# A list scheduler's price for changing the tensor engine's array mode, and new due times, in a four-layer transformer kernel

## The chip, the cores and the metric

The kernel runs on one core of a Trainium2 chip. The metric is the device time of the program in microseconds; the time of a kernel is the median of several runs. The engines are called TensorE (PE), VectorE (DVE), ScalarE (ACT), GpSimd (POOL) and SyncE (SP, which issues transfers); PEld is the loading of weights into TensorE.

## The reference

Eight sequences of 512 x 512 numbers pass through four layers. Each layer is `x = x + layernorm(f(layernorm(x)))`, with these four functions `f`:

```python
# 1: attention without weights, on each of the 8 sequences
weights = softmax(einsum('bci,bcj->bij', x, x)); out = einsum('bij,bcj->bci', weights, x)
# 2: eight 512 x 512 factors, summed by linearity, then a bias
out = einsum('btd,rde->bte', x, factors) / sqrt(8) + bias
# 3: RMS norm, 8 query heads of 64 in 2 groups that share keys and values, output projection
h = norm_scale * x / (norm(x) / sqrt(512) + eps) * split_scale
q, k, v = h @ Wq.T, h @ Wk.T, h @ Wv.T
out = x + softmax(q @ k.T / 8) @ v @ Wo.T
# 4: gated feed-forward with 1408 hidden units and ternary weights
out = (silu(x @ gate_w.T * gate_s) * (x @ up_w.T * up_s)) @ down_w.T * down_s
```

All numbers are float32.

## The kernel before

The 8 sequences are called batches 0 to 7. Each has four token tiles of 128 rows. Per batch there are four stages: `stage_attn0` (names that begin with a0), `stage_ffn0` (f0), `stage_attn1` (a1; for the last batch its attention rows, products and projections are named e1) and `stage_ffn1` (f1; h1 for the last batch, where the first gate products are split into two halves of the tokens). TensorE does the following in them:

- a0: transposes of the normalized x (L635), the upper half of the score matrix (L693, and transposes L691 for the rest), transposes of the softmax rows (L635), context products (L724).
- f0, for each token tile: four transposes of a normalized row (L609), eight matmul instructions against the summed factors (L746).
- a1: transposes (L635), keys (L885), values (L896), queries (L915); then, for four pairs of heads and two halves of the tokens, scores (L944), transposes of the softmax rows (L975), attention products (L1006), and the output projections (L1032).
- f1: transposes (L635), gate and up products (L1165, eight instructions each), down products (L1233).

TensorE works in four modes, by which the planner tells operations apart: "128x128" is whole float32 work (L609, L693, L724, L746, L885, L896, L915, L1032), "64x128" is work on two halves of the array's rows (L635, L944, L975), "128x64" on two halves of its columns (L1006), and "128x128r" is whole work on float32r operands (L1165, L1233). In float32r a value is split into two parts, which are multiplied by weights that are exact in it. A flag that is computed from the weights' low bits (the "low" loads and L463) tells whether this holds; otherwise the whole program runs again in float32.

No order of instructions is written out by hand. Each stage hands its operations to a `Recorder` with an engine, an estimated duration, the buffers that it reads and writes, and a priority. `Recorder.issue` then puts them in order: again and again it looks, for each engine, at the operations that could start within SLACK of the earliest, and takes the one with the smallest due time. An operation that needs another mode than the engine is in starts later by `Recorder.change`, and its due time counts as later by STAY times that. The order so found is the order in each engine's queue[...]. Due times come from `due`: the table DUE holds for each kind of work a start and steps, in units of one batch, and SHIFT adds an offset for a stage and a batch; SMALL is taken off for operations under 0.3 us.

Buffers are rings: 5 banks f and 3 banks g of PSUM, 4 tiles e for softmax rows, 3 tiles row, 2 tiles hl, and 4 tiles each of ws (weights of a1, loaded on SP's queue) and wgu (gate and up weights, loaded on POOL's queue, L387). A buffer is taken when the operation that first needs it is put in order, so that order also decides when loads can start. The statistics of a normalization take DVE (L516, L521), then POOL (L525, L532), then DVE again (L540); the addition to x is on POOL (L559).

Of the kernel before, what the change touches and what calls it, by code (L numbers as in the profile page):

```python
# [53 lines left out]
class Recorder:  # L54
# [4 lines left out]
    @staticmethod  # L59
    def change(eng, old, new):  # L60


        if new is None or new == old:
            return 0.0
        if eng == "ACT":
            return 1.3
        return 0.09 * (old is None or old.strip("r") != new.strip("r")) + 0.12 * new.endswith("r")

    def __init__(self):
        self.ops = []  # L70
# [2 lines left out]
    def add(self, eng, dur, fn, reads=(), writes=(), room=(), after=(), state=None, lat=None):  # L73
# [5 lines left out]
        op.lat = self.LAT[eng] if lat is None else lat  # L79
        op.prio = self.prio - (SMALL if dur < 0.3 else 0.0)  # L80
        op.succ, op.wait, op.ready = [], 0, 0.0
# [34 lines left out]
    def issue(self, places, slack):  # L116
# [24 lines left out]
        while left:  # L141
            best = None
            for e, ops in ready.items():
# [3 lines left out]
                first = min(able)[0]  # L147
                stay = STAY.get(e, 0.0)
                pick = min(
# [99 lines left out]
def layers(  # L249
# [1034 lines left out]
    with tc.manual_schedule():  # L1284
        rec.issue(places, SLACK)

# [1 line left out]


DUE = {  # L1290
    "x": (-2.595,),
    "fsum": (0.4631, 0.0036),
    "scales": (-1.7557,),
    "wd": (0.2919,),
    "low": (0.8154, 1.1722),
    "a0.norm": (0.602,),
    "a0.row": (-0.0133, 0.0064),
    "a0.out": (0.6155, 0.0012),
    "f0": (-0.2291, 0.103),
    "a1.norm": (0.498, -0.0333),  # L1300
    "a1.kv": (-2.1194,),
    "a1.q": (0.5487, 0.0684),
    "a1.row": (0.5193, 0.0805, 0.0215, -0.0006),
    "a1.mix": (1.3287, 0.0052, 0.0124),
    "a1.out": (1.6207, -0.0361),
    "e1.row": (0.4681, -0.0113, 0.0525, -0.0529),
    "e1.mix": (-2.4837, 58.3341, 0.0746),
    "e1.out": (1.1439, 0.155, 0.0456),
    "f1.norm": (-0.1878, 0.009),
    "f1.gate": (1.5586, 0.0013),  # L1310
    "f1.down": (1.7415, 0.1322, 0.0313),
    "h1.norm": (1.5393, -1.0876, 0.0495),
    "h1.gate": (2.1757, 0.4491, 4.54),
    "h1.down": (1.6071, -1.5421, 1.3412),
}

SHIFT = {
    ("a0", 0): 0.0119,
    ("a1", 0): -0.3641,
    ("f0", 0): 0.0009,  # L1320
    ("f1", 0): -0.1337,
    ("x", 0): 0.0116,
    ("a0", 1): 0.0009,
    ("a1", 1): -0.1282,
    ("f0", 1): -0.3583,
    ("f1", 1): -0.001,
    ("x", 1): 0.0094,
    ("a0", 2): 0.0721,
    ("f1", 2): -0.0021,
    ("x", 2): 0.3533,  # L1330
    ("a1", -2): -0.0219,
    ("f0", -2): -0.0106,
    ("f1", -2): -0.0418,
    ("x", -2): -0.0328,
    ("a0", -1): 0.0045,
    ("a1", -1): -0.1019,
    ("f0", -1): 0.0436,
    ("f1", -1): 0.0947,
}

STAY = {"PE": 0.1755}

SLACK = {"PE": 0.123, "ACT": 0.0985, "DVE": 0.0676, "POOL": 0.7848, "SP": 0.1357}

SMALL = 0.8265
FSUM_POOL = (0, 3)
EARLY = (-1,)
FEW = 4
# [54 lines left out]
```

## Time and profile before

| | us |
|---|---|
| median of 3 runs | 1516.56 (1516.08 to 1517.06) |
| profiled execution | 1518.21 |
| its span, first to last instruction | 1516.3 |
| TensorE busy in it | 1472.7 |
| VectorE busy | 1052.4 |
| ScalarE busy | 671.1 |
| GpSimd busy | 578.6 |
| first matmul starts at | 15.9 |
| last matmul ends at | 1506.7 |

The span leaves 1.9 us of the profiled execution around it. "Busy" is the union of an engine's instructions; for TensorE the ends of matmuls are modelled, so idle time that the profile shows on it is a lower bound of what it lost. In a timeline, each line gives the start, the length, the engine, the line of the program, the operation with what it writes and reads, the number of merged instructions, and in brackets the idle time before it and what ended that. In a list of waits, the numbers are the total, the count and the longest.

### The profile page before, as it was taken

To read this page: it belongs to the slowest core of one execution; us is meant where nothing else is said; L and a number is where in the kernel's file an instruction comes from. 1 tells how busy PE (TensorE), PEld (TensorE's weight loads), DVE (VectorE), ACT (ScalarE), POOL (GpSimd) and SP (SyncE) were. 2 spreads that over 40 slices of the span, in tenths; PEclk is the share of its full clock that TensorE was granted. 3 is DMA by queue.
4 is the path that set the end of the run, shared out by engine and by line. 5 is a ranking of instruction groups with operands and counts; after the bars stand their busy time and mean duration, and the time that the engine had idled before them with its cause. 6 is when DMAs were issued, how large, how long until landed. Compare 5 with 4: busy or idle time off the path is not lost.

```text
span 1516.3 us, 23151 instructions
## 1 busy us (share of the span) xinstructions
PE 1472.7 (97%) x8562; PEld 909.2 (60%) x8562; DVE 1052.4 (69%) x2227; ACT 671.1 (44%) x1426; POOL 578.6 (38%) x884
## 2 busy tenths in 40 slices
PE   5999999999999999999999999999999999999997
PEld 3444557655766557665566656665566655666575
DVE  6899865768558685586846868466774757748745
ACT  3226645642276414663256622565325642266312
POOL 6661142236412374033721347103571116602341
PEclk9999999999999999999999999999999999999999
DMA  9523046112521214212151122411233103420281
GB/s 335 158 84 112 2 105 112 36 42 49 98 63 43 48 44 91 56 48 65 29 104 36 57 56 49 97 37 43 56 70 84 36 15 77 77 63 22 56 161 38
DMA packets 156698, 108.04 MB, mean 71 GB/s; under 512 B 7072, under 2 KB 137120, under 8 KB 156576
## 3 DMA queue, kind: packets, MB, share of 16 engines
q0 software_dynamic: 98736, 51.13, 17.9%
q1 hardware_dynamic: 57840, 55.34, 11.5%
q8 instruction: 70, 1.15, 0.3%
q14 instruction: 52, 0.43, 0.1%
HBM read 98.06 MB, written 8.39 MB: 70 GB/s over the span
## 4 chain that ended last, share of the span: by engine, by line
PE 80%; DVE 9%; POOL 6%; DMA 2%; issue 2%; SPq 0%; ACT 0%; POOLq 0%; DVEq 0%; ACTq 0%
PE g L1165 18%; PE g L1233 11%; PE f L944 7%; PE f L1006 7%; PE f L915 7%; PE f L1032 6%; PE f L724 6%; PE f L975 5%; PE f L693 4%; PE f L746 3%; PE f L635 2%; POOL rstd L532 2%; PE f L896 2%; PE f L885 2%; DVE row L540 1%
## 5 line engine op out<-in xcount | busy, mean ns | idle before, releaser
L1165 PE MATMUL g<-hl,wgu 128*128 128x512 f32 (+1 forms) x1408 | 339.3, 394 | 1.9 <-DMA wgu<-in_gate_t 1.7
L1165 PEld LDWEIGHTS g<-hl,wgu 128*128 128x128 f32 x1408 | 256.7, 189 | 71.9 <-DVE s L573 10.6
L525 POOL TENSOR_SCALAR ve<-mv 128x1 f32<-128x1 f32 x224 | 62.5, 280 | 591.6 <-DVE mv L521 584.4
L573 DVE TENSOR_REDUCE s<-f 128x1 f32<-128x512 f32 x288 | 184.9, 684 | 107.3 <-PE f L944 66.5
L580 ACT ACTIVATE e<-f,s 128x512 f32<-128x512 f32 x288 | 195.9, 688 | 76.5 <-DVE s L573 73.3
L559 POOL TENSOR_TENSOR x<-x,z 128x512 f32<-128x512 f32 x120 | 163.8, 1368 | 48.2 <-DVE z L540 42.7
L1233 PE MATMUL g<-wd,hl 128*128 128x512 f32 x704 | 174.8, 401 | 1.4 <-DVE hl L1108 1.4
L987 ACT COPY big<-f 128x512 f32<-128x512 f32 x256 | 135.9, 593 | 71.8 <-PE f L975 71.5
L1233 PEld LDWEIGHTS g<-wd,hl 128*128 128x128 f32 x704 | 129.4, 188 | 52.3 <-issue 20.7
L597 DVE TENSOR_SCALAR e<-e,s 128x512 f32<-128x512 f32 x288 | 145.3, 508 | 8.4
L532 POOL TENSOR_TENSOR rstd<-ve,mhalf 128x1 f32<-128x1 f32 x224 | 142.0, 638 | 16.0
L387 POOL DMA_DIRECT2D wgu<-in_up_t x92 | 75.0, 815 | 151.1 <-PE g L1165 146.6
L944 PE MATMUL f<-kv,big 64*128 64x512 f32 x512 | 131.2, 613 | 0.1
L1195 DVE SCALAR_TENSOR_TENSOR sig<-g,gs,sig 128x512 f32<-128x512 f32 x84 | 62.7, 747 | 87.4 <-ACT sig L1185 87.1
L1006 PE MATMUL f<-big,kv 128*64 128x256 f32 x1024 | 122.6, 384 | 0.0
L1032 PE MATMUL f<-ws,big 128*128 128x512 f32 x256 | 116.6, 600 | 0.7 <-ACT big L870 0.7
L746 PE MATMUL f<-fsum,rT 128*128 128x512 f32 x256 | 115.7, 595 | 0.2
L915 PE MATMUL f<-big,ws 128*128 128x512 f32 x256 | 115.5, 599 | 0.0
L724 PE MATMUL f<-big,big 128*128 128x512 f32 x256 | 114.8, 597 | 0.0
L1185 ACT ACTIVATE sig<-g,gs 128x512 f32<-128x512 f32 x84 | 58.6, 698 | 119.4 <-PE g L1165 99.6
L387 POOL DMA_DIRECT2D wgu<-in_gate_t x92 | 72.6, 790 | 99.9 <-PE g L1165 93.3
L1204 DVE SCALAR_TENSOR_TENSOR hd<-g,us,sig 128x512 f32<-128x512 f32 x84 | 62.8, 747 | 67.0 <-PE g L1165 63.8
(91 smaller groups left out, 1920.2 us busy)
## 6 DMA issues: line engine op xcount, KB each, us to landing
wgu<-in_gate_t POOLq DMA_DIRECT2D x92, 256.0 KB, 3.3
wgu<-in_up_t POOLq DMA_DIRECT2D x92, 256.0 KB, 3.3
x<-in_x SPq DMA_DIRECT2D x32, 256.0 KB, 2.6
ws<-in_wq_t SPq DMA_DIRECT2D x32, 256.0 KB, 3.3
ws<-in_wo_t SPq DMA_DIRECT2D x32, 256.0 KB, 2.6
out<-x SPq DMA_DIRECT2D x32, 256.0 KB, 2.0
hd<-in_factors SPq DMA_DIRECT2D x28, 256.0 KB, 5.3
wd<-in_down_t POOLq DMA_DIRECT2D x11, 256.0 KB, 8.4
```

The source lines that it names most:

```text
L532: lambda: nc.gpsimd.tensor_tensor(rstd.t[:, :], ve.t[:, :], mhalf, ALU.pow),
L559: lambda: on.tensor_tensor(ap(xt), ap(xt), y.t[:, :], ALU.add),
L573: lambda: nc.vector.tensor_reduce(nmax.t[:, :], sc.t[:, :], AX.X, ALU.max, negate=True),
L580: lambda: nc.scalar.activation(e.t[:, :], sc.t[:, :], AF.Exp, bias=nmax.t[:, :], accum_out=tot.t[:, :]),
L724: nc.tensor.matmul(po.t[:, :], xnT.t[:, j, ts(t, P)], wT.t[:, j, :], start=(j == 0), stop=(j == KT - 1),)
L746: nc.tensor.matmul(po.t[:, :], xnT.t[:, kt, :], fsum.t[:, kt, :], start=(kt == 0), stop=(kt == KT - 1),)
L915: nc.tensor.matmul(pq.t[:, :], wq.t[:, kt, :], hT.t[:, kt, :], start=(kt == 0), stop=(kt == KT - 1),)
L944: nc.tensor.matmul(scs[g].t[:, :], qT.t[gp, i, ts(s, P)], kT.t[gp, :], start=True, stop=True,)
L1006: nc.tensor.matmul(po.t[gp, : 2 * P], v.t[:, t * P + g * DH : t * P + (g + 1) * DH], columns_of(aT)[:, g * NT + t, :], start=(t == 0), sto ...
L1032: nc.tensor.matmul(po.t[:, :], qT.t[:, i, ts(t, P)], flat(wos[i].t), start=(i == 0), stop=(i == NPAIR - 1),)
L1165: nc.tensor.matmul(bank.t[:, cut], w.t[:, kt, :], d.t[:, kt, cut], start=(n == 0), stop=(n == KT * len(xs) - 1),)
L1233: nc.tensor.matmul(po.t[:, :], ap(o)[:, it - lo, :], wd.t[:, it, :], start=(it == 0 and k == 0), stop=(it == NI - 1 and k == len(ops) - 1),)
```

## The change

The function that prices a change of mode on TensorE is given other prices. Before, a change between "128x128" and "128x128r" cost 0.12 us into float32r and 0 out of it, a change from tiled work to float32r cost 0.21, and any other change 0.09. After, a change between "128x128" and "128x128r" costs 0 in both directions, and every other change costs 0.21 into float32r and 0.09 elsewhere. All due times, the offsets by batch, STAY, three of the SLACK values and SMALL get new values. No operation, buffer, duration or transfer is added or taken away. The line numbers of the kernel after are larger by 2 from L67 on.

```diff
-        return 0.09 * (old is None or old.strip("r") != new.strip("r")) + 0.12 * new.endswith("r")
+        if old is not None and old.strip("r") == new.strip("r"):
+            return 0.0
+        return 0.21 if new.endswith("r") else 0.09
...
-    "f0": (-0.2291, 0.103),
-    "a1.norm": (0.498, -0.0333),
-    "a1.kv": (-2.1194,),
-    "a1.q": (0.5487, 0.0684),
-    "a1.row": (0.5193, 0.0805, 0.0215, -0.0006),
-    "a1.mix": (1.3287, 0.0052, 0.0124),
...
+    "f0": (-0.1636, 0.1196),
+    "a1.norm": (0.4967, -0.0502),
+    "a1.kv": (-1.8548,),
+    "a1.q": (0.5431, 0.0591),
+    "a1.row": (0.5193, 0.0765, 0.0294, -0.0187),
+    "a1.mix": (1.4217, -0.005, 0.0185),
...
-STAY = {"PE": 0.1755}
-
-SLACK = {"PE": 0.123, "ACT": 0.0985, "DVE": 0.0676, "POOL": 0.7848, "SP": 0.1357}
-
-SMALL = 0.8265
+STAY = {"PE": 0.0901}
+
+SLACK = {"PE": 0.123, "ACT": 0.0528, "DVE": 0.0772, "POOL": 1.2606, "SP": 0.1357}
+
+SMALL = 0.8159
```

The other entries of DUE and SHIFT change in the same manner.

More of the change, by code (lines that the diff above doesn't have):

```diff
@@ L1290 @@
 DUE = {
[L1291 to L1298, printed above, removed]
-    "f0": (-0.2291, 0.103),
-    "a1.norm": (0.498, -0.0333),
-    "a1.kv": (-2.1194,),
-    "a1.q": (0.5487, 0.0684),
-    "a1.row": (0.5193, 0.0805, 0.0215, -0.0006),
-    "a1.mix": (1.3287, 0.0052, 0.0124),
-    "a1.out": (1.6207, -0.0361),
-    "e1.row": (0.4681, -0.0113, 0.0525, -0.0529),
@@ L1307 @@
[L1307 to L1314, printed above, removed]
+    "x": (-2.3159,),
+    "fsum": (0.3241, 0.0093),
+    "scales": (-1.7199,),
+    "wd": (0.1588,),
+    "low": (0.6749, 1.0396),
+    "a0.norm": (0.5999,),
+    "a0.row": (-0.0925, 0.0032),
@@ new lines @@
+    "a0.out": (0.61, 0.0014),
+    "f0": (-0.1636, 0.1196),
[4 more added lines that the diff above has]
+    "a1.mix": (1.4217, -0.005, 0.0185),
+    "a1.out": (1.6212, -0.0623),
+    "e1.row": (0.2868, -0.0014, 0.037, -0.0171),
+    "e1.mix": (-2.6369, 42.9472, 0.5484),
+    "e1.out": (1.0638, 0.0783, 0.0342),
+    "f1.norm": (-0.7064, 0.0727),
+    "f1.gate": (1.5542, 0.001),
+    "f1.down": (1.7443, 0.1972, 0.0317),
@@ L1315 @@
+    "h1.norm": (1.3712, -0.2677, 0.0575),
+    "h1.gate": (2.6762, 0.5726, 5.4087),
+    "h1.down": (1.5597, -2.5384, 1.2861),
 }
 SHIFT = {
[L1318 to L1338, printed above, removed]
-}
-STAY = {"PE": 0.1755}
-SLACK = {"PE": 0.123, "ACT": 0.0985, "DVE": 0.0676, "POOL": 0.7848, "SP": 0.1357}
-SMALL = 0.8265
+    ("a0", 0): -0.0077,
+    ("f0", 0): 0.3239,
+    ("f1", 0): -0.0869,
+    ("a0", 1): -0.1846,
+    ("a1", 1): -0.1496,
+    ("f0", 1): -0.3089,
+    ("x", 1): -0.0564,
+    ("a0", 2): 0.3238,
+    ("a1", 2): -0.0022,
+    ("f0", 2): 0.0353,
@@ L1346 @@
+    ("f1", 2): -0.0044,
+    ("x", 2): 0.0586,
+    ("a1", -2): -0.0031,
+    ("f0", -2): 0.1802,
+    ("f1", -2): -0.0946,
+    ("x", -2): -0.3405,
+    ("a0", -1): -0.0302,
+    ("a1", -1): -0.1096,
+    ("f0", -1): -0.4004,
+    ("f1", -1): -0.1873,
+    ("x", -1): 0.1371,
+}
+STAY = {"PE": 0.0901}
+SLACK = {"PE": 0.123, "ACT": 0.0528, "DVE": 0.0772, "POOL": 1.2606, "SP": 0.1357}
+SMALL = 0.8159
 FSUM_POOL = (0, 3)
```

## The prediction

> **What bounds the kernel now.** I read the page first: busy shares, granted clock, chain.
>
> ```profile
> span 1516.3 us, 23151 instructions
> PE 1472.7 (97%) x8562; PEld 909.2 (60%) x8562; DVE 1052.4 (69%) x2227; ACT 671.1 (44%) x1426; POOL 578.6 (38%) x884
> ...
> PEclk9999999999999999999999999999999999999999
> ...
> PE 80%; DVE 9%; POOL 6%; DMA 2%; issue 2%; SPq 0%; ACT 0%; POOLq 0%; DVEq 0%; ACTq 0%
> ```
>
> TensorE (PE) is busy 97% of the span, at full clock in every slice, and is most of the chain. The span is therefore PE's work, plus what a change of array mode costs, plus PE's waits. The diff leaves the matmuls alone, so only the last two can move. Next, PE's waits over the span, and the places where the largest stand in the PE timeline:
>
> ```profile
> PE f L635 <- DVE big L540: 15.9, 1, 15.9
> PE f L609 <- DVE row L540: 4.2, 6, 0.9
> PE f L635 <- DVE z L540: 2.0, 2, 1.6
> PE g L1165 <- DMA wgu<-in_gate_t: 1.7, 3, 0.9
> ```
>
> ```profile
> 558.62 2.07 PE L1165 MATMUL g<-hl,wgu 128*128 128x512 f32 x8
> 560.53 3.59 PE L746 MATMUL f<-fsum,rT 128*128 128x512 f32 x8
> 564.99 0.66 PE L609 MATMUL f<-ident,row 128*128 128x128 f32 x4 [0.86 <-DVE row L540]
> ```
>
> ```profile
> 164.80 1.11 PE L944 MATMUL f<-kv,big 64*128 64x512 f32 x4
> 165.71 0.22 PE L975 MATMUL f<-ident,e 64*128 64x64 f32 x1
> 166.13 1.01 PE L975 MATMUL f<-ident,e 64*128 64x64 f32 x15 [0.20 <-ACT big L987]
> 166.98 2.29 PE L944 MATMUL f<-kv,big 64*128 64x512 f32 x4
> 169.20 1.95 PE L1006 MATMUL f<-big,kv 128*64 128x256 f32 x16
> ```
>
> 15.9 us is the start, before the first operand. Ends of matmuls are modelled, so I measure a wait from start to start. At 560.53 a feed-forward product of the first layer (L746) takes 4.46 us until the next transposes start, where others take 3.43 to 3.58: a loss of 0.95 (0.86 shown as idle). It recurs in batches 3, 4, 5 and 6 (564.99, 748.41, 931.51, 1114.58): 3.8 us. In the second fence, two score products (L944) keep PE 2.22 us instead of 1.03, because the product behind them (L1006) waits for copies; no idle is printed, since the modelled end is stretched. Six such places between 159 and 179 us lose 0.35, 0.86, 0.72, 1.19, 0.86 and 0.76: 4.7 us.
>
> [...] Over all neighbours in the PE timeline, start to start less what the same products take among their like, a change from tiled work (64x128 or 128x64) to float32r costs 0.23 us, tiled to whole 0.20, float32r or whole to tiled 0.15, between the two tilings 0.15 to 0.17; between whole float32 and float32r it is 0.00 to 0.02. [...] after the start no wait is above 1.6 us and the granted clock is 0.996, so the clock is no second lever. [...] L540 took 1.55 us beside a GpSimd add (L559, 1.26 us from 563.39), against 0.57 for the rows of the later normalization.
>
> **The change part by part.** It edits no instruction; it alters the planner's price of a PE mode change, due times, STAY, SLACK and SMALL, and all of these act through the order alone. I compared the two orders, engine by engine. PE's first 37 operations are the same, and its last 47 (from 1419.5 us on: the last attention products and projections, the split gates, the last down products). So the 15.9 us start, the other waits before 97 us, the waits for wgu near the end and the 1.36 us one at 1484 stay. SP keeps 203 of 215 places and moves no entry by more than 7; POOL's wgu loads keep their sequence, four of them stand earlier between its small operations near 1420 us.
>
> *Mode changes.* Before: 461; 67 between whole and float32r (free), 394 paid. After: 470; 75 free, 395 paid. By kind: tiled to float32r 71 to 72 (+0.23 us); tiled to whole 82 to 82; 128x64 to 64x128 49 to 47 (-0.3), 64x128 to 128x64 40 to 41 (+0.2); float32r to tiled 75 to 72 (-0.45), whole to tiled 77 to 81 (+0.6). Sum +0.3. Priced by single lines rather than by mode, I get -0.6. I take 0, range -0.6 to +0.3. The new price is nearer to the measured ones, but its effect on the number of paid changes is nil.
>
> *First feed-forward, batches 2 to 7.* The row of the fourth token tile hangs on the last context product (L724) through two normalizations on DVE and POOL. I add up the PE work between that product and the transposes that need the row (cover). Before: 17.5 us in batches 3 to 6, which stall; 21.5 and 21.1 in batches 2 and 7, which don't. After: two gate products (L1165, 1.9 each) move ahead of these transposes, cover is 21.1 in batches 3 to 7, and 17.5 in batch 2. Four losses go, one comes: -3 x 0.95 = -2.85. What is late next: in the new order DVE writes the row only after the bias (0.68) and statistics (0.69, 0.18) of the third tile, so about 2.1 to 3.6 us after the third product (the row at 0.57 or at 1.55), against 3.8 us of gate products. It fits barely: at worst 0.3 each, +1.5.
>
> *Attention of batch 0, 159 to 179 us (4.7 us lost).* Feed-forward products, keys of batch 1 and transposes are interleaved with it otherwise. Covers in the new order: an attention product (L1006) behind its transposes has 1.1 us once and 1.6 twice (before, 1.1 three times, losing 0.86, 1.19, 0.86, so about 2.0 is needed): +0.9 and +0.4; the other 1.6 follows the wait named next, which covers it. One set of softmax transposes (L975) stands only 1.0 us behind its scores; before, 3.5 was the shortest and did not stall: up to +2.5. The values' weights (wv, L896) reload a ws buffer that the keys (L885) free, with 2.6 us of PE work between; ws loads land 2.5 to 5.8 us after issue, median 2.8, and the SP queue has nothing unfinished ahead: about +0.4. Sum 4.2 against 4.7: -0.5. Bounds: -3 if the softmax is covered by what PE has already waited for, +2.5 if as much again is exposed.
>
> *Batch 2 (339 to 361 us).* Transposes of batch 3 (L635 at 354.1) wait 0.6 for a bank that ACT empties, and others cost 0.3 at 342.7. Afterwards the first stand among gate products with 7.9 us before the next context product, the others behind another projection: -1.0, between -1.2 and 0.
>
> *Last attention (1336 to 1428 us).* The second projection of the early half moves ahead of the last down product. Its transposes at 1427.4 lost 0.33 and a softmax at 1366.9 0.2; both get more cover: -0.4.
>
> Sum: 0 - 2.85 - 0.5 - 1.0 - 0.4 = -4.75 us. The profiled execution took 1518.21 (span 1516.3 and 1.9 around it), so 1513.5 for the like after; the median of the runs, 1516.56, is 1.65 lower, so 1511.8.
>
> **The rivals.** (a) *Waits move.* Each gain needs the non-PE engines to keep pace, and cover says nothing of queues on DVE and POOL. If the fourth row stays late (+1.5) and batch 0 loses 2 more, -1.3 is left: 1515.3. For it: the new DVE order puts that row later. Against: batch 7 of the old kernel has the same 21.1 us and no wait. (b) *Slower: the ws ring between batches 0 and 1.* Four ws buffers serve, one behind the other, wv, the first wq, the last wo and the second wq, each load waiting for the PE product before; their covers are 2.6, 3.7, 3.9 and 3.9 us, where before no such reload had under 12. At the longest landing seen, 5.8, they lose 3.2 + 2.1 + 1.9 + 1.9 = 9.1 instead of 0.4: +8.7 - 4.75 = +4, 1520.5. It passes zero once landing and release exceed about 5 us in all four. Against: the median is 2.8, and the check loads (hd) ahead of these in the SP queue are issued by then. (c) *Better than forecast:* batch 0 is covered nearly wholly (-3 instead of -0.5): 1509.3. (d) *The price does not do what it says:* paid changes stay at 395 instead of falling; that is in the sum.
>
> **How the numbers follow.** What a measurement can tell from no change is about 0.2%, 3.0 us: faster means below 1513.5, slower above 1519.6. The forecast with its own bounds, 1508.5 to 1513.5, has 0.52; (c) 0.18; (a), 1513.5 to 1519.6, 0.20; (b) 0.10. Faster 0.70, same 0.20, slower 0.10. The range for 8 in 10 runs from 1507.5 (c with its bounds) to 1517.0, leaving out (b) and the end of (a).
>
> **What would show it.** Right: no wait of L609 for row L540 near the third product in batches 3 to 6, one in batch 2; paid changes still cost the same each; first 97 and last 90 us alike. Wrong: L609 still waiting in batches 3 to 6; L896, L915 or L1032 waiting for a ws transfer between 170 and 200 us; L975 waiting more than 2.5 us for a row of e in batch 0; new PE waits in batch 1, where gate products of batch 0 are spread otherwise.

## The result, and the profile after

| | before | after |
|---|---|---|
| median, us | 1516.98 (20 runs, 1516.08 to 1519.52) | 1515.74 (20 runs, 1513.89 to 1517.54) |
| profiled execution, us | 1518.21 | 1514.31 |
| span of it, us | 1516.3 | 1512.4 |
| mean granted clock over it | 0.996 | 0.998 |

The ratio is 0.9991, 95% interval [0.9984, 0.9998]: 1.24 us gained, where 4.75 us were forecast. A second set of runs (21 of after, 30 of before) gave 1515.84 against 1517.12 and the same ratio and interval. The two profiled executions differ by 3.9 us, three times as much. Executions of one kernel differ in how often the clock of TensorE falls to half for 3.41 us: before's profile has two such windows inside its work (at 60.31 and 1446.12 us, granted clock 0.50), after's none, and the mean clock of 104 executions of before goes from 0.995 to 0.999. The medians decide, and the profiles are read operation by operation.

The page of after, to be held against the lines of before in the prediction:

```profile
span 1512.4 us, 23159 instructions
PE 1468.9 (97%) x8562; PEld 907.7 (60%) x8562; DVE 1050.5 (69%) x2227; ACT 665.7 (44%) x1422; POOL 586.2 (39%) x884
...
PE 86%; DVE 5%; POOL 4%; issue 2%; DMA 1%; ACT 1%; SPq 0%; POOLq 0%; DVEq 0%; ACTq 0%
```

The bound is the same: TensorE, 97% busy. Its waits over the span (the engine, its line, what it waited for; total, count, longest; lines are larger by 2 than in before):

```profile
PE f L637 <- DVE big L542: 15.9, 1, 15.9
PE f L611 <- DVE row L542: 3.4, 7, 1.1
PE f L637 <- DVE z L542: 2.0, 2, 1.6
...
PE f L977 <- ACT big L872: 0.8, 2, 0.5
...
PE f L917 <- DVE z L761: 0.7, 1, 0.7
```

The wait of the first feed-forward for its row (4.2 us in six places before) has fallen by 0.8 only, and several waits of the second attention are new: the last two lines here, and six more of 0.2 to 0.6 us each. The timeline of TensorE in the first feed-forward of batch 3 shows why the first line fell so little:

```profile
550.08 3.59 PE L748 MATMUL f<-fsum,rT 128*128 128x512 f32 x8
553.88 0.66 PE L611 MATMUL f<-ident,row 128*128 128x128 f32 x4 [0.20 <-DVE row L542]
...
561.95 3.59 PE L748 MATMUL f<-fsum,rT 128*128 128x512 f32 x8
...
569.03 0.60 PE L611 MATMUL f<-ident,row 128*128 128x128 f32 x4
```

The fourth row (569.03) has no wait any more, as forecast. The second row (553.88) has one that before did not have; from start to start it costs 0.35 us, in each of batches 3 to 6.

With the same operations of both programs set side by side, after minus before in start time is +0.3 us at the first keys of batch 0 (101 us), +1.2 at the attention of batch 2 (467 us), 0.0 in batch 3 (627), -0.8, -1.7 and -2.5 in batches 4, 5 and 6, and -2.65 when the last gate products start (1435). So the change loses 0.9 us in batches 0 to 2, gains 3.7 in the first feed-forwards of batches 3 to 6 and 0.15 in the last attention. That makes -2.9; the medians show -1.24. Two questions follow: what is lost early, and what takes the other 1.6 us.

### The profile page after: what moved, and what is told of

Read it like the earlier page. It is cut to its first block, busy times and chain, and to the rows that moved or that the text cites. A ratio compares the mean times of both kernels' runs of the same rounds, so it can differ in the third digit from the quotient of the medians.

```text
span 1512.4 us, 23159 instructions
## 1 busy us (share of the span) xinstructions
PE 1468.9 (97%) x8562; PEld 907.7 (60%) x8562; DVE 1050.5 (69%) x2227; ACT 665.7 (44%) x1422; POOL 586.2 (39%) x884
## 4 chain that ended last, share of the span: by engine, by line
PE 86%; DVE 5%; POOL 4%; issue 2%; DMA 1%; ACT 1%; SPq 0%; POOLq 0%; DVEq 0%; ACTq 0%
PE g L1167 21%; PE g L1235 11%; PE f L1008 8%; PE f L946 8%; PE f L917 7%; PE f L1034 7%; PE f L977 5%; PE f L726 5%; PE f L748 5%; PE f L695 4%; PE f L637 2%; PE f L898 2%; PE f L887 2%; POOL rstd L534 1%; DVE row L542 1%
## 5 line engine op out<-in xcount | busy, mean ns | idle before, releaser
L527 POOL TENSOR_SCALAR ve<-mv 128x1 f32<-128x1 f32 x224 | 67.8, 304 | 593.1 <-DVE mv L523 587.0
L977 PEld LDWEIGHTS f<-ident,e 64*128 64x128 f32 x2048 | 73.3, 139 | 52.5 <-issue 40.7
```

## The experiments

Most kernels here issue a given order: a subclass of `Recorder` takes the operations by number from a list, and takes buffers as `issue` does. They have the line numbers of before. All comparisons are with runs of before on the same chip.

### One half of the change at a time

At operation 1900 of the 5152 that the program records, in the attention of batch 2, both orders have done the same set of operations, so they can be joined there.

```diff
-    rec = Recorder()
+    rec = Forced()
...
+ORDER = order_of_before[:1900] + order_of_after[1900:]   # kernel "late"
+ORDER = order_of_after[:1900] + order_of_before[1900:]   # kernel "early"
```

> Edit: the order of operations of before up to a point in the attention of batch 2 at which both orders have done the same operations, and the order of after from there on. Theory A (the change gains in the first feed-forward of batches 3 to 6 and at the last attention, and loses in batches 0 to 2): the same operations start 3.8 us earlier by the last attention than in before (2.65 us there in after, plus the 1.17 us that after had lost by the start of batch 3), so about -3.8 us against before, 1513.2 us. Rival B (the small measured gain of after is spread over the whole program or is a matter of the clock of single executions): about half of after's gain, -0.6 us, 1516.4 us.

> Edit: the reverse: the order of after up to the same point in batch 2, the order of before from there on. Theory A: the loss alone, +1.17 us against before, about 1518.2 us. Rival B: about -0.6 us, 1516.4 us. The differences of this run and of the run with the late half, added, should give after's own -1.2 us only if the two halves don't act on each other: theory A says -3.8 + 1.2 = -2.6 us, 1.4 us more gain than the medians of before and after show, and puts that down to the clock.

Measured: late 1513.44 against 1516.78, ratio 0.9977 [0.9967, 0.9987], -3.3 us. Early 1519.41, ratio 1.0016 [1.0009, 1.0022], +2.6 us. Together -0.7, near after's own -1.2. Theory A holds in signs and for the late half; rival B falls. The early half costs twice what theory A took from start times. In the profiled execution of early, which had no half-clock window before its last products and was the fastest of the 21, the operations of batch 3 start only 0.9 us later than in before, counted from the first keys, as in after. The rest of the 2.6 us is not in that profile; the part on the clock takes it up.

### The row beside the addition on POOL

DVE and POOL at the second row of the first feed-forward in batch 4, first before, then after (timelines; merged neighbours have a count):

```profile
733.99 1.60 POOL L532 TENSOR_TENSOR rstd<-ve,mhalf 128x1 f32<-128x1 f32 x3
734.60 0.55 DVE L540 TENSOR_SCALAR row<-x,mv,rstd 128x512 f32<-128x512 f32 x1 [2.51 <-POOL rstd L532]
...
736.60 1.30 POOL L559 TENSOR_TENSOR x<-x,z 128x512 f32<-128x512 f32 x1 [1.00 <-DVE z L540]
```

```profile
734.00 0.57 POOL L534 TENSOR_TENSOR rstd<-ve,mhalf 128x1 f32<-128x1 f32 x1
734.54 1.26 POOL L561 TENSOR_TENSOR x<-x,z 128x512 f32<-128x512 f32 x1
734.60 1.48 DVE L542 TENSOR_SCALAR row<-x,mv,rstd 128x512 f32<-128x512 f32 x1 [2.35 <-POOL rstd L534]
```

The row starts at the same moment, and takes 0.55 us in one kernel and 1.48 in the other, where POOL begins its addition at 734.54. The new order moved the addition ahead of two roots. Two kernels exchange neighbours on POOL in batches 3 to 6, and nothing on the other four engines:

```diff
 POOL's queue, kernel late_pool (late, and this in a0/f0)
-x<-x,z (L559)   rstd (L532)
+rstd (L532)     x<-x,z (L559)
 POOL's queue, kernel before_pool (order of before, and this in f0)
-x<-x,z (L559)   s<-s,half (L830)
+s<-s,half (L830)   x<-x,z (L559)
```

> Edit: the kernel with before's order early and after's late, and in the first feed-forward of batches 3 to 6 one swap on POOL: the 1.26 us addition to x moves behind the next reciprocal square root, so that the normalization of the second row on DVE (L540) no longer runs beside it. Theory C (the new wait of 0.35 us in each of the four batches is the row stretched from 0.55 to 1.48 us by the addition on POOL beside it): 4 x 0.35 = 1.4 us less than without the swap, about -5.2 us against before, 1511.8 us, and the row at 0.55 us. Rival D (the row is late because its own mean and root come late, and its length does not matter): no difference to the kernel without the swap, 1513.2 us.

> Edit: the order of before with nothing on PE, DVE, ACT or SP changed; on POOL alone, in the first feed-forward of batches 3 to 6, the addition to x (1.26 us) goes behind the halving of an RMS sum (0.55 us) that followed it: four swaps of two neighbours. Theory C: the row of the fourth tile, 1.55 us beside that addition, takes 0.55 us, and the wait of 0.95 us of TensorE in each of the four batches goes without any product being moved ahead: about -3.8 us against before, 1513.2 us, as much as the whole late half of the change. Rival D: the row stays late, 0 to -0.4 us, 1516.8 us; a middle result (-1.4 us) would mean that the row meets the addition in part.

Measured: late_pool 1511.41, ratio 0.9961 [0.9948, 0.9975], -5.4 us. Before_pool 1512.67, ratio 0.9972 [0.9962, 0.9983], -4.1 us. The slowest of the five late_pool runs (1512.17) is below the fastest of the nine of late (1512.88), so the swap itself is worth 2.0 us, more than the 1.4 of theory C. Theory C holds in both, rival D falls. In before_pool, the fourth row of batch 4:

```profile
745.14 0.76 POOL L830 TENSOR_TENSOR s<-s,half 128x1 f32<-128x1 f32 x1
745.31 0.55 DVE L540 TENSOR_SCALAR row<-x,mv,rstd 128x512 f32<-128x512 f32 x1
745.65 1.34 POOL L559 TENSOR_TENSOR x<-x,z 128x512 f32<-128x512 f32 x1
...
745.91 0.66 PE L609 MATMUL f<-ident,row 128*128 128x128 f32 x4
```

In before, the same two stand like this, DVE ahead of POOL:

```profile
746.80 1.55 DVE L540 TENSOR_SCALAR row<-x,mv,rstd 128x512 f32<-128x512 f32 x1
746.81 1.26 POOL L559 TENSOR_TENSOR x<-x,z 128x512 f32<-128x512 f32 x1
```

A row that starts together with the addition, as here, takes about 1.5 us; with the halving put between, it leads by 0.34 us and takes 0.55, although the addition still begins before it ends. TensorE's transposes at 745.91 have no wait any more. Four swaps on an engine that is 38% busy bring 4.1 us, over three times what the whole change brings. The changed order had got around the late row by putting products ahead of its transposes; that hides the slow row and leaves it slow.

### Price alone, due times alone

> Edit: the new price of a change of form alone, with the old due times. Its order is before's up to place 200 of 841 on TensorE (all of batches 0 and 1); in the first feed-forward of batches 3 to 6 it moves two products ahead of the fourth row's transposes, as after does, and its POOL takes both roots ahead of the addition there, as before does. Theory A with C (early half as in before costs nothing, the row is not late): the gain of the late half with POOL's order mended, -4 to -5.4 us against before, about 1512 us, and a mean clock of 0.997 to 0.998 in most executions. Rival E (old due times don't suit the new price, so that waits appear elsewhere): -1 to +1 us, 1516 to 1517.5 us.

> Edit: the new due times alone, with the old price. Its order is after's in nearly every place up to 150 of TensorE and through batches 1 to 6. Theory A: the loss of the early half and the new 0.35 us wait come from the due times, so it lands where after does, -0.5 to -2 us against before, 1515 to 1516.3 us, at a mean clock of 0.995 to 0.996. Rival E: due times and price suit each other only together, and it is slower than before by 1 us or more.

The edits are the first hunk of the diff alone (price) and all but the first hunk (tables).

Measured: price 1513.03 against 1517.26, ratio 0.9973 [0.9962, 0.9983], -4.2 us. Theory A with C holds. TensorE pays for 397 changes of form, three more than in before, so the price gains through the order of the first feed-forward and not through the count. Of the waits for a row there (waits of TensorE in price, whole span), only two are left, and both stand before 68 us, so none is in batches 3 to 6:

```profile
PE f L611 <- DVE row L542: 0.9, 2, 0.5
```

Tables 1527.94, ratio 1.0063 [1.005, 1.0076], +10.7 us: rival E. Its order falls apart where those due times meet the old price, for instance (waits of TensorE in tables, 395 to 410 us, then 1300 to 1470 us):

```profile
PE g L1165 <- DMA wgu<-in_gate_t: 1.7, 1, 1.7
```

```profile
PE f L635 <- DVE row L540: 2.8, 3, 1.3
PE f L1165 <- DMA wgu<-in_up_t: 1.7, 3, 1.0
PE g L1165 <- ACT hl L1099: 1.2, 1, 1.2
```

So the due times undo 3 us of what the price alone would bring, and without the price they make the kernel slower by 10.7 us. Which of these waits weighs most in tables was not tested.

### What holds TensorE in batch 0's attention

By the reckoning of the prediction (start to start, less what the same operations take elsewhere), TensorE loses 6.7 us between 150 and 183 us in after, against 4.7 in before; and 0.8 us at 113 us, where before lost nothing. TensorE is busy for this much of two stretches of 10 us (from:to, length, busy us and count of PE, PEld, DVE, ACT and POOL, granted clock, share of the DMA engines, GB/s), in before and then in after:

```profile
155.00:165.00 10.00, 9.81 (x98) 5.14 (x96) 8.68 (x23) 7.02 (x20) 3.72 (x6) 1.00 0.01 2
165.00:175.00 10.00, 9.61 (x82) 4.56 (x82) 9.61 (x30) 8.64 (x22) 1.85 (x4) 1.00 0.01 2
```

```profile
155.00:165.00 10.00, 8.51 (x94) 4.98 (x92) 9.52 (x29) 8.04 (x23) 4.80 (x8) 1.00 0.10 18
165.00:175.00 10.00, 8.67 (x99) 5.35 (x100) 9.46 (x22) 9.34 (x29) 0.00 (x0) 1.00 0.16 39
```

Three suspects were tried in four kernels: DVE's ORs of the weights' low bits, moved (after_or) or left out with their loads (after_no_low); ACT's scaled copies of batch 1, of which after_copy writes a quarter, so that three quarters of batch 1's normalized rows are missing in it; the order of the rows on TensorE (after_t3).

```diff
 after_or: ten ORs (L463) and the flag, from TensorE's places 82 to 93 to places 92 to 103
 after_no_low:
-            load(raw[0], ...)
+            add("SP", 0.85, lambda: None, writes=[raw])
...
-                nc.vector.tensor_tensor(bits(), bits(), ..., ALU.bitwise_or)
+                pass
 after_copy (L870):
-                    for kt in range(KT):
+                    for kt in range(1 if b == 1 else KT):
 after_t3, TensorE's queue:
-T(a1.norm.1)  tr6  tr7  sc8  mix  k  tr8  sc  sc  v  tr  mix  tr  q  mix
+tr6  sc8  tr7  mix  T(a1.norm.1)  tr8  sc  sc  k  tr  mix  v  tr  mix  q
```

(T: transposes of batch 1's normalized x, tr: softmax transposes, sc: scores, mix: attention product, k, v and q: keys, values and queries; numbers are the row pairs of batch 0.)

> Edit: the order of after, with ten ORs of the look at the low bits (L463 of before, L465 of after; 0.69 us each on DVE) and what follows from them moved from the last rows of batch 0's attention (167 to 182 us) to behind it (185 to 205 us). Theory O (these ORs stand in DVE's queue ahead of the softmax maxima, and TensorE waits for the rows): the stretch loses 1.0 to 2.0 us less, about -1.5 us against after, 1514.2 us, and the mean clock rises to 0.997 or more[...]. Rival L (the four scaled copies of L872, 1.15 us each on ACT, and TensorE's own order hold the stretch): 0 to -0.3 us against after, 1515.6 us.

> Edit: the order of after with the 33 loads and the 33 ORs of the look at the low bits left out (the flag is then made from zeros, so that part of the check isn't done). Theory O: both places go, the 0.8 us at 113 us, where five ORs stand ahead of a bias addition, and 1.0 to 2.0 us at 167 to 182 us: -2 to -2.8 us against after, 1513.3 us. Rival L: only the 0.8 us, 1514.9 us. A gain over 3.5 us would mean that the loads of the look delay the weights as well.

> Edit: the order of after; of the four chunks of each scaled copy of batch 1's first norm on ACT (L870 of before, L872 of after, 1.15 us a copy) only the first is written, so that each copy takes about 0.3 us; three quarters of batch 1's normalized rows are left out with that. Theory L (these copies stand in ACT's queue ahead of batch 0's exponentials and copies of rows, and hold TensorE's stretch from 155 to 183 us): the stretch loses about 6 us in after, of which 1.0 to 2.0 us go, 1514.0 to 1514.7 us, and the half-clock windows there become rarer. Rival S (the order of the rows on TensorE itself makes the chain: maxima on DVE, exponentials on ACT, transposes, with too little beside them): 0 to -0.4 us, 1515.5 us.

> Edit: the order of after; in batch 0's attention, between 169 and 196 us, the scores of the seventh row pair (L944 of before, L946 of after) go ahead of the transposes of the eighth, and batch 1's second norm transposes (L635/L637), which hold two of the five PSUM banks f, go from ahead of these scores to behind the next attention product; keys, values and the first query of batch 1 follow two to four places later. Theory R (what holds this stretch is the order of the rows on TensorE together with the banks: a score pair that starts 2 us later gives a softmax that ends 2 us later): 1.5 to 3.5 us of the some 6 us lost from 155 to 183 us go, 1512.3 to 1514.3 us, TensorE is busy for 9.3 or more of the 10 us from 165 to 175 (8.7 in after), and mean clocks of 0.997 to 0.998 become more frequent. Rival F (the chain of maxima, exponentials, copies and transposes has its length whatever the order): within 0.5 us of after, 1515.3 to 1516.3 us.

Measured: after_or 1522.83 against 1517.26, ratio 1.0029 [1.0019, 1.004], +5.6 us, against after's -1.2. The ORs are not what holds the stretch: its waits are those of after, to 0.02 us each, where the clock is full. First after, then after_or, waits of TensorE from 150 to 185 us:

```profile
PE f L977 <- ACT big L872: 0.8, 2, 0.5
PE f L977 <- DVE e L599: 0.6, 1, 0.6
PE f L977 <- ACT e L582: 0.5, 1, 0.5
PE f L946 <- ACT e L582: 0.4, 1, 0.4
```

```profile
PE f L975 <- ACT big L870: 0.8, 2, 0.5
PE f L975 <- DVE e L597: 0.6, 1, 0.6
PE f L975 <- ACT e L580: 0.5, 1, 0.5
PE f L944 <- ACT e L580: 0.4, 1, 0.4
```

DVE, freed of the ORs there, is busy for 5.99 of the 10 us from 165 (after_or; 9.46 in after):

```profile
165.00:175.00 10.00, 8.68 (x88) 5.24 (x88) 5.99 (x16) 7.87 (x23) 0.00 (x0) 0.84 0.11 31
```

The loss of after_or comes from where the move ended. The one matmul that sums up these bits (L476) stands in TensorE's queue and now waits for the ORs, and a projection behind it for its bank (waits in 100 to 230 us):

```profile
PE f L476 <- DVE s L471: 2.7, 1, 2.7
PE f L1032 <- DVE z L1047: 1.4, 1, 1.4
```

After_no_low, 1513.76, ratio 0.9979 [0.997, 0.9987], -3.5 us, 2.3 better than after. It keeps the stretch's waits unchanged, so for the stretch theory O falls twice. What goes is the 0.8 us at 113 us, as expected, and 1.3 us at 92 us, which both kernels lose and which has its own experiment below. That the time comes near theory O's 1513.3 us is luck: the gain stands elsewhere than it said.

After_copy, 1514.67 against 1517.12, ratio 0.9983 [0.9973, 0.9992]. The interval reaches into that of after run beside it (1515.84, [0.9984, 0.9998]). In its trace the stretch loses 6.2 us instead of 6.7: the 0.8 us for L872 is gone, and longer waits for exponentials (L944 0.9 instead of 0.4, L896 0.5 instead of 0.2) bring most of it back. So the trace gives theory L 0.5 us of the 1 to 2 it expected. The median is 1.2 us below that of after, at the edge of theory L's range; the other 0.7 us is not in the trace and was not assigned.

After_t3, 1519.11 against 1516.67, ratio 1.0016 [1.0009, 1.0024], +2.4 us. Neither theory R nor rival F expected that. Scores that start earlier didn't give a softmax that ends earlier (waits in 100 to 230 us):

```profile
PE f L975 <- DVE e L597: 3.8, 4, 1.3
PE f L975 <- DVE s L590: 1.1, 1, 1.1
PE f L1006 <- ACT big L987: 1.1, 1, 1.1
```

The rows now wait for their normalization on DVE, whose queue still holds the ORs (ten of them between 172 and 181 us). So it stays open which link sets this stretch in after. The ORs are excluded as its main cause, and the copies account for 0.5 of its 6.7 us; that it is the order of the rows was not shown.

### The clock

> Edit: none; the order of after, run again. Theory W (the early half of after leaves TensorE so thin in batch 0's attention, 155 to 183 us, that in most executions the clock falls to half there for one or two windows of 3.41 us, at up to 1.7 us each): 1515.7 us against 1517 us of before; a mean clock of 0.995 to 0.996 in most executions, against 0.998 of before; and a profile at 0.996 or less shows the windows between 160 and 180 us. Rival (the clock falls at chance places in all kernels alike): the same distribution of mean clocks as before, windows elsewhere.

The edit is none. Measured: 1515.84 against 1517.12, ratio 0.9991 [0.9984, 0.9998]. Theory W holds. The profile of this execution has a mean clock of 0.995. Its clock record has half clock for 6.83 us from 61.28 us, and for 3.41 us from 173.92 (windows of TensorE, as above):

```profile
165.00:175.00 10.00, 8.68 (x92) 4.97 (x90) 9.46 (x22) 9.51 (x28) 0.00 (x0) 0.95 0.22 55
175.00:185.00 10.00, 10.00 (x49) 4.25 (x48) 7.89 (x16) 4.27 (x12) 0.00 (x0) 0.88 0.09 26
```

In after_or, which is after up to 167 us, there are two in the stretch, at 164.07 and 174.31 us, and a third where L476 waits, at 218.69. Tables has the same two, at 164.25 and 174.49; after_no_low one at 170.21. Of the eight profiles with after's early order or one near it, four have such a window between 160 and 180 us; of the six with before's, none. In after_or the operations in either window take 1.64 us longer than the same ones at full clock. Over all executions, the mean clock of before was 0.998 or more in 67 of 104, of after in 3 of 41; after's most frequent value is 0.996 (24 of 41). The mean is 0.9975 and 0.9961. Of some 1514 us, 0.0014 is 2.1 us of full clock: the author's upper estimate of what the median loses, as the two windows of after_or cost 1.64 us each, a little under half of their 3.41 us. That fits the 1.6 us that the start times leave open, and the 1.7 us of early that its profile did not show.

Executions with the same mean clock can be compared directly. At 0.998, before takes 1516.9 us (mean of 66), after 1513.6 (3) and early 1518.0 (1): -3.3 and +1.1 us, near the -2.9 and +0.9 of the start times. At 0.996, after takes 1516.1 (24) and before 1517.2 (15). The executions at 0.998 are few, but they say the same as the traces.

Where the windows fall is in the record too. Within one profile they begin at whole multiples of 3.413 us from each other (406 of them in before, 3 and 13 in after_or). All fourteen profiles together have fifteen places of half clock before 1500 us, and each begins right behind a window of the same length in which TensorE was busy for only 25 to 67%. These are the windows just before 173.92 in after_again, and before 164.07 and 174.31 in after_or:

```profile
170.51:173.92 3.41, 2.28 (x35) 1.71 (x35) 3.27 (x9) 3.41 (x11) 0.00 (x0) 1.00 0.17 62
```

```profile
160.66:164.07 3.41, 2.05 (x29) 1.47 (x26) 3.27 (x12) 2.76 (x8) 2.22 (x4) 1.00 0.04 7
170.90:174.31 3.41, 2.28 (x35) 1.71 (x35) 2.05 (x7) 3.41 (x11) 0.00 (x0) 1.00 0.03 7
```

From 150 to 183 us, the emptiest stretch of 3.413 us, wherever it is laid, is 80% busy in before and 60% in after. Such a window did not always bring half clock: over thirty others of 52 to 67% passed at full clock, one of them in after itself (159.95, 2.18 us busy). After_t3 has the thinnest stretch of all (TensorE busy for 7.66 of the 10 us from 165, and 7.84 of the 10 from 175) and no half clock there (1.00 in both). So a window of at most 67% came before every fall here; what more it takes was not found.

### A version that beats both, and a try at more

Late_pool (1511.41) beats both kernels. One more meeting of DVE and POOL stands on the path of before, late and late_pool alike, at 92 us, and was moved apart in the kernel best:

```diff
 POOL's queue, a0.out of batch 1 (late_pool, and this)
-x<-x,z (L559)   ...   ve (L525)
+ve (L525)   x<-x,z (L559)     # the moments that read x follow, on DVE too
```

> Edit: the kernel with before's early half, after's late half and POOL's four swaps, and one more move in batch 1's first attention at 92 us: the addition to x on POOL (1.27 us) goes behind the next variance step, with the moments that read its result. A DVE operation of one column (L839) takes 1.21 us beside that addition, and 0.2 us elsewhere, and the row that waits for it holds TensorE for 1.1 us. Theory C: that wait goes as well, -1.0 us, 1510.4 us, about -6.4 us against before. Rival D: the row is late anyway, or the moved moments hold the next feed-forward's first row: 0 to +1 us, 1511.4 to 1512.4 us.

Measured: 1511.40 against 1517.12, ratio 0.9963 [0.9949, 0.9976], -5.7 us; not to be told from late_pool. The operation of one column in before, and in best:

```profile
91.16 1.21 DVE L839 SCALAR_TENSOR_TENSOR s<-s,rstdl,rms_eps 128x1 f32<-128x1 f32 x1 [0.26 <-POOL s L830]
```

```profile
90.52 0.22 DVE L839 SCALAR_TENSOR_TENSOR s<-s,rstdl,rms_eps 128x1 f32<-128x1 f32 x1 [0.26 <-POOL s L830]
```

It shrank as theory C said, and the loss at 92 us fell from 1.3 to 0.3 us. It is given back 20 us later (waits in best, 80 to 130 us), by a softmax. TensorE begins its scores 2.0 us earlier than in late_pool (109.73 against 111.77), DVE its maximum only 1.0 us earlier (113.44 against 114.45), with nine ORs of the low bits in a row ahead of it. Theory C's further 1.0 us doesn't show; rival D had the right time, and the loss in another place:

```profile
PE f L975 <- DVE s L590: 0.7, 1, 0.7
```

## Why the prediction was right or wrong

The measured median lies in the range, but in its upper end, and "within 0.2%", which came true, had only 0.20; 0.70 stood on faster. The likeliest case, -4.75 us, was wrong by 3.5 us. By the steps of the sum:

- **Mode changes, 0.** Not contradicted. Changes that occur at least four times in both traces cost the same in both to 0.01 us, and 395 are paid against 394. By the prices taken from before, the operations and changes of after sum to 1463.5 us against 1464.1: -0.6, the lower bound that was given. That is a reckoning; no run measures this term alone.
- **First feed-forward, -2.85.** The mechanism was right: the fourth row's waits in batches 3 to 6 are gone, and one of 0.86 us came in batch 2. By start times 1.2 us were gained in batch 3 and 0.8 in each of the other three, 3.7 in all, and with the 0.86 lost that is -2.8: the sum came out, in part by luck. The second row got a wait of 0.35 us in each of the four batches, so 0.6 each was to be expected; what gave the rest there was not traced. The prediction asked what is late next and looked at the fourth row only. It had seen the row of 1.55 us beside the addition on POOL, and did not ask where the new order puts those additions for the other rows. Nor did it price the remedy that before_pool then showed.
- **Batch 0's attention, -0.5, bounds -3 and +2.5.** This is the term that failed: +2.0 by waits, and 0.8 at 113 us besides. (By start times, after has lost 1.3 us more at 344 us than at 101; the rest of the 2.8 is made up between, by what was not traced.) The sum went by cover, TensorE's work between a product and what needs it, with answer times of DVE and ACT taken from before. It had no term for transposes that wait for ACT's copies of batch 1 (0.8 us in the trace) and none at 113 us, where a bias addition stands behind ORs on DVE. In the stretch DVE and ACT are busy for 9.5 and 8.0 to 9.3 of 10 us, but full queues are not shown to be the reason: in after_or DVE is busy for 6.0 of the 10 us from 165, with the same waits. Rival (a) said this in words ("cover says nothing of queues on DVE and POOL") and had 1515.3 us, nearest to what was measured, with a chance of 0.20.
- **Batch 2, -1.0, and the last attention, -0.4.** The waits of 0.88 and 0.30 us in batch 2 went as said. The last attention gave 0.15.
- **"The clock is no second lever."** Wrong: about 1.6 us by difference. The argument was that no wait after the start is above 1.6 us; that this is enough for full clock was the author's assumption, and the traces contradict it. In the four profiles with half clock between 160 and 180 us, no gap of TensorE there is longer than 0.61 us, and the windows of 3.41 us just before are 60 to 67% busy. Nor did the prediction ask why the profile of before had shown 0.996, a mean below full clock.
- **Rival (b), the ws ring.** The values start 0.8 us late at 183 us (182.65), where 0.4 was forecast. Their weights had landed at 182.35, and the trace puts the end of that wait down to an exponential on ACT, so the ring's share of it is not shown. The other three reloads cost next to nothing. It did not decide. Rival (d): the count stayed where it was (394 before, 395 after); the price gained all the same (price alone, -4.2 us), by moving two products.

The two terms that went wrong, batch 0's attention and the clock, hide a gain that is real: the late half alone is -3.3 us, with POOL mended -5.4, about what was forecast for the whole.

## What to carry to other kernels

When a reordering shortens one wait, list every operation of the partner engines that it moves next to a contended one: four exchanges of two neighbours on a GpSimd that is 38% busy were worth over three times the whole change (a row of 0.55 us on DVE took 1.5 beside an addition there). Cover counted in TensorE time was wrong here by 2.5 us in one stretch of 30 us, twice the gain that was measured; give such a term a range of its own size, and ask for each answering engine what stands ahead in its queue. Judge a difference as small as this one (1.24 us, 0.1%, where single executions of before lie up to 3.4 us apart) by medians of many runs, compare executions of the same mean clock, and cut two orders at a common point to see which half gains.

## What the runs showed of the hardware that had not been expected

- TensorE's clock falls to half for 3.413 us inside work: in fourteen profiles, fifteen times before 1500 us, always right behind a window of that length in which TensorE was 25 to 67% busy, and in batch 0's attention with no gap above 0.61 us. It happens in some executions of a program and not in others (after's profile has none, mean clock 0.998; after_again's, of the same kernel, has 6.83 us of it from 61.28 us and 3.41 from 173.92, mean 0.995); about 1.64 us were lost for each in after_or.
- Which DVE operations a POOL addition (1.26 us) holds up, and from when. In seven traces (before, after, late, late_pool, before_pool, price, best) 106 rows of 512 columns (L540, from x to row; 0.55 us alone) began between 0.04 us ahead of an addition and 0.94 us into it. Every one ended 0.28 to 0.29 us behind the addition, so that it took up to 1.59 us. The 27 that led by 0.09 us or more took 0.53 to 0.55. The operation of one column (L839) began 0.06 to 0.07 us into an addition 13 times, and ended 0.01 to 0.02 us behind it each time (1.20 to 1.22 us, 0.22 otherwise). The statistics of 512 columns (L516), 185 times beside an addition, were not held: 0.70 us at most. So rows which by the record start up to 0.04 us ahead of the addition were held all the same, and those that lead by 0.09 us were not; no row between the two was seen.
